# Scan inputs as two three-buffer tiles, four residual tiles and earlier loads in a four-layer transformer, LoRA, Mamba and mixture-of-experts kernel

## The chip, the cores and the metric

The kernel runs on one core of one Trainium2 chip. The metric is the device time of one execution in microseconds (us), shown as the median of several executions. A profile is one further execution, recorded by the hardware profiler. Its span reaches from the first to the last recorded instruction.

## The reference, cut to what matters

The input is 4 sequences of 1024 tokens with 256 features, all float32. Four blocks follow each other, each as `x = x + layernorm(f(layernorm(x)))`:

```
f1: x*16 + position; 4 layers of linear attention (16 heads) and a 256-1024-256 feed-forward; final layernorm
f2: x @ W.T + LoRA mixture of 8 experts of rank 16, gated by a softmax
f3: Mamba: xz = x @ W_in (256 -> 2 x 512); causal conv of 4 taps; silu;
    delta = softplus(dt @ W_dt + b);   per channel d and state s (16):
    h[t] = h[t-1] * exp(delta[t,d] * A[d,s]) + (delta*u)[t,d] * B[t,s];   y[t,d] = sum_s h[t] * C[t,s]
    y = (y + xc * D) * silu(z);  out = layernorm(x + y @ W_out)
f4: top-1 mixture of 8 experts (256-1024-256), 320 slots each
```

The recurrence over `t` is the scan that this document is about. It is done for 4 sequences x 512 channels x 16 states.

## The kernel before, in words

**Tiling.** The tokens are cut into 8 blocks of 512 (`TB`), two blocks to a sequence. A block of activations is a tile of 128 partitions x 4 x 256 (512 KB, 4 KB a partition). 32 units (block, layer) of the transformer run as a software pipeline: the loop at L1279 goes over steps `u`, and in each step it calls parts of several units: `a_norm`, `a_turn`, `a_query`, `a_keys` for unit u+3, `a_sums` for u+2, `b_heads`, `b_turn`, `b_out`, `b_turn2` for u+1, and `f_up`, `f_down` for u. Two sequences are in work at a time, so up to four blocks hold a residual tile `X[j]`. When a block has passed its last layer, `c_norm` (u-1) reads `X[j]` for the last time, and `c_add` to `c_open` do the LoRA part. `init(j)` (L281), called at the start of step u for unit u+4 when that unit is of layer 0, loads the input `xt` and the position table `pos`, normalizes `xt`, and makes `X[j]` (L288, five buffers, tag "X"). `a_norm` for that unit comes one step later.

**Between the parts** `pump` (L1268) draws pieces of a second stream, with a credit of 34 to 42 per step: for each block `front(j)` (Mamba's projections, the convolution, delta; stores to DRAM), `scan(j)`, `back(j)` (the output projection), `route(j)`, and near the end the experts. When the steps are over, what is left of the stream runs alone.

**Front.** `turn` (L698) transposes the block, then `project(0)` and `project(1)` (L710) each take a buffer of tag "t4" (three buffers), load half of `w_in` (512 KB, L712) and multiply at once (L716). L763 to L795 compute delta and delta*u and store them as `dud` in DRAM, one after the other for each channel.

**Scan.** 128 partitions are 16 channels x 8 states, so a block has 32 groups of 16 channels, each with two halves of the states (k = 0, 1). For each group one DMA (L842, issued on SP's queue) reads 16 channels of `dud` and repeats each over 8 partitions into `dd`, 128 x 2 x 512: delta in `dd[:, 0]`, delta*u in `dd[:, 1]`. Tag "dd" has two buffers; in the last two blocks every third group takes the free weight buffer "wkv" in its place. Then for each k: GpSimd (POOL) multiplies `dbu = dd[:, 1] * B` (L848, three buffers), ScalarE (ACT) does `h = exp(A * dd[:, 0])` into PSUM (L850, two buffers), VectorE (DVE) runs the scan instruction (L854), saves the last column (L858) and multiplies by C (`hc`, L860, nine buffers), and TensorE (PE) sums over the states (L818). The `dd` buffer is free when both POOL and ACT have read it for k = 1.

**Experts.** Every second expert holds its two halves of w1, and every expert its result `ye`, in buffers of tag "X".

**What sets the order.** A scheduler of the framework puts the instructions of each engine into one fixed order when the kernel is built: it takes what is ready in its own estimate, earliest in the program first, and gives out the buffers in that order. On the chip each engine works through its order strictly, and so does SP, which issues nearly all DMAs: an instruction or a DMA that waits holds up all that stand behind it in its queue.

Of the kernel before, what the change touches and what calls it, by code (L numbers as in the profile page):

```python
# [17 lines left out]
P = 128  # L18
D = 256
# [47 lines left out]
def sandwich_kernel(ctx: ExitStack, tc: tile.TileContext, io: dict):  # L67
# [145 lines left out]
    def layers(ctx: ExitStack):  # L213
# [64 lines left out]

        X = {}

        def init(j):  # L281

            xt = tok(f"xt{j}")
            nc.sync.dma_start(xt, xblock(x_in, j))
            pos = tok(f"pos{j}")
            nc.sync.dma_start(pos, xblock(io["pos"], j % NB))
            norm_on_act(xt, xt)
            X[j] = xres.tile([P, NT, D], F32, tag="X", name="X", bufs=5)  # L288
            nc.vector.scalar_tensor_tensor(X[j], xt, math.sqrt(D), pos, ALU.mult, ALU.add)

        S = [dict() for _ in units]
        KV = {}
# [402 lines left out]
        def front(j):  # L695

            mcol = m["mcol"]
            uT = turn(closed.pop(j), pool=fpool, tag="t4", bufs=3)  # L698
            yield 0
            xc = fpool.tile([P, NDB, TB], F32, tag="xc", name="xc")  # L700
            stores = []

            def store(dst, src):
                stores.append((dst, src))

            def flush():
                while stores:
                    nc.sync.dma_start(*stores.pop(0))

            def project(part):  # L710
                w = fpool.tile([P, NC_D, D_IN], F32, tag="t4", name="win", bufs=3)
                nc.sync.dma_start(w, io["w_in"][:, :, part * D_IN : (part + 1) * D_IN])  # L712
                for db in range(NDB):
                    ps = mm([P, TB], "psx")
                    for kc in range(NC_D):
                        nc.tensor.matmul(  # L716
                            ps,
                            w[:, kc, db * P : (db + 1) * P],
                            uT[:, kc, :],
                            start=kc == 0,  # L720
                            stop=kc == NC_D - 1,
                        )
                    yield db, ps

            def sigmoid(src):

                s = fpool.tile([P, TB], F32, tag="sg", name="sg", bufs=2)
                nc.scalar.activation(s, src, AF.Exp, scale=-1.0)
                nc.scalar.activation(s, s, AF.Ln, bias=1.0)
                nc.scalar.activation(s, s, AF.Exp, scale=-1.0)  # L730
                return s

            for db, ps in project(0):
                w = mcol[:, db, M_W : M_W + 4]
                xi = fpool.tile([P, TB + 3], F32, tag="xi", name="xi")
                if j % NB == 0:
                    nc.gpsimd.memset(xi[:, 0:3], 0.0)
                else:
                    nc.gpsimd.tensor_copy(xi[:, 0:3], m["hist"][:, db, :])
                nc.scalar.copy(xi[:, 3 : TB + 3], ps)  # L740
                nc.scalar.activation(
                    ps, ps, AF.Identity, bias=mcol[:, db, M_CB : M_CB + 1], scale=w[:, 3:4]
                )
                if j % NB == 0:
                    nc.gpsimd.tensor_copy(m["hist"][:, db, :], xi[:, TB : TB + 3])
                for k in range(3):
                    nc.vector.scalar_tensor_tensor(
                        ps, xi[:, k : k + TB], w[:, k : k + 1], ps, ALU.mult, ALU.add
                    )
                s = sigmoid(ps)  # L750
                nc.vector.tensor_tensor(xc[:, db, :], s, ps, ALU.mult)
                store(xcd[j][db], xc[:, db, :])
                yield 2.1
                flush()
            for db, ps in project(1):
                s = sigmoid(ps)
                nc.vector.tensor_tensor(s, s, ps, ALU.mult)
                store(zsd[j][db], s)
                yield 0.8
                flush()  # L760
            ps = mm([P, TB], "psd")
            for c in range(NDB):
                nc.tensor.matmul(  # L763
                    ps, m["w_x"][:, c, :], xc[:, c, :], start=c == 0, stop=c == NDB - 1
                )
            dbc = fpool.tile([P, TB], F32, tag="dbc", name="dbc")
            nc.scalar.copy(dbc, ps)
            for side in range(2):
                for h in range(NSH):
                    r = side * 32 + DT_RANK + h * SH  # L770
                    store(bcd[j][side, :, h, :], dbc[r : r + SH, :])
            yield 0
            flush()


            for db in range(NDB):
                ps = mm([P, TB], "psdt")
                o = db * 32
                nc.tensor.matmul(
                    ps, m["w_dt"][o : o + DT_RANK, :], dbc[o : o + DT_RANK, :], start=True, stop=True  # L780
                )
                bdt = mcol[:, db, M_BDT : M_BDT + 1]
                du = fpool.tile([P, 2, TB], F32, tag="t4", name="du", bufs=3)
                e, lv = du[:, 0, :], du[:, 1, :]
                v1 = fpool.tile([P, TB], F32, tag="sg", name="v1", bufs=2)
                nc.scalar.activation(e, ps, AF.Abs, bias=bdt)
                nc.scalar.activation(ps, ps, AF.Relu, bias=bdt)
                nc.scalar.activation(e, e, AF.Exp, scale=-1.0)
                nc.scalar.activation(lv, e, AF.Ln, bias=1.0)
                nc.vector.tensor_scalar(v1, e, 1.0, -1.0, ALU.add, ALU.add)  # L790
                nc.gpsimd.tensor_tensor(v1, e, v1, ALU.subtract)
                nc.gpsimd.tensor_tensor(v1, v1, lv, ALU.add)
                nc.vector.tensor_tensor(ps, v1, ps, ALU.add)
                nc.scalar.copy(du[:, 0, :], ps)
                nc.vector.tensor_tensor(du[:, 1, :], xc[:, db, :], ps, ALU.mult)  # L795
                store(dud[j][db], du)
                yield 2
                flush()

        def scan(j):  # L800
# [12 lines left out]
            for db in range(NDB):  # L813
# [13 lines left out]
                for r in range(GQ):  # L827
# [6 lines left out]
                    for q in range(4):  # L834
                        g = q * GQ + r
                        gg = db * (P // GC) + g
                        if j >= NBLK - 2 and g % 3 == 2:

                            dd = wpool.tile([P, 2, TB], F32, tag="wkv", name="dd")
                        else:  # L840
                            dd = spool.tile([P, 2, TB], F32, tag="dd", name="dd", bufs=2)
                        nc.sync.dma_start(  # L842
                            dd,
                            dud[j][db][g * GC : (g + 1) * GC].unsqueeze(1).to_broadcast([GC, SH, 2, TB]),
                        )
                        for k in range(NSH):
                            dbu = spool.tile([P, TB], F32, tag="dbu", name="dbu", bufs=3)
                            nc.gpsimd.tensor_tensor(dbu, dd[:, 1, :], Bt[:, k, :], ALU.mult)  # L848
                            h = ps_h.tile([P, TB], F32, tag="h", name="h")
                            nc.scalar.activation(  # L850
                                h, dd[:, 0, :], AF.Exp, scale=m["A"][:, gg, k : k + 1]
                            )
                            last = m["last_h"][:, gg, k : k + 1]
                            nc.vector.tensor_tensor_scan(  # L854
# [199 lines left out]
        def expert(k, e=None):  # L1054
# [12 lines left out]
                row = e * CAP  # L1067
                which = slice(e, e + 1)
            if k % 2:
                w1 = [xres.tile([P, NC_D, FF // 2], F32, tag="X", name="ew1", bufs=5) for _ in range(2)]  # L1070
                w2 = apool.tile([P, NFC, D], F32, tag="kv", name="ew2", bufs=1)
            else:
                w1 = [wpool.tile([P, NC_D, FF // 2], F32, tag=t, name="ew1") for t in ("w1a", "w1b")]
                w2 = wpool.tile([P, NFC, D], F32, tag="w2", name="ew2")
# [33 lines left out]
            for f in range(NFC):  # L1108
# [11 lines left out]
                nc.scalar.activation(hT[-1][:, f % 4, :], ps, AF.Relu)  # L1120
                if f % 2:
                    yield 0
            ye = xres.tile([P, NCK, D], F32, tag="X", name="ye", bufs=5)
            both = mm([P, 2, D], "pse")
            last = ps_kv.tile([P, NC_D, P + 1], F32, tag="kv", name="psk").rearrange(
                "p c m -> p (c m)"
# [150 lines left out]
        init(0)  # L1277
        load(0, "cols", "wq", "wkv", "rkv")
        for u in range(-3, len(units) + 4):  # L1279
            if at(u + 4) and u > -4 and units[u + 4][1] == 0:  # L1280
                init(units[u + 4][2])
            if u == 2:
                load_lora()
            if u == 4:
# [3 lines left out]
            def add(func, n, *args, when=at):  # L1288
                if when(n):
                    parts.append(lambda: func(n, *args))  # L1290

            add(a_norm, u + 3)
            add(a_sums, u + 2)
            add(f_up, u, 0)
            add(c_norm, u - 1, when=last_layer)
            add(c_open, u - 3, when=last_layer)
            parts.append(lambda: load(u + 1, "w1a"))
            add(b_heads, u + 1)
# [16 lines left out]
            parts.append(lambda: load(u + 4, "cols", "wq", "wkv", "rkv"))  # L1315
            add(c_gate, u - 1, when=last_layer)
            add(b_turn2, u + 1)
            for part in parts:
                part()
                pump(SSM_RATE[min(len(begun), 2)] / len(parts))  # L1320
# [110 lines left out]
```

## Time and profile before

| | |
|---|---|
| median of 3 executions | 2957.96 us (2955.56 to 2959.54) |
| the profiled execution's own time | 2954.41 us |
| its span | 2952.6 us |
| mean granted TensorE clock | 0.910 |
| PE busy | 2459.1 us (83%) |
| DVE busy | 1867.6 us (63%) |
| ACT busy | 1541.6 us (52%) |
| POOL busy | 1121.7 us (38%) |
| first and last scan instruction (DVE L854) | 801.7 and 2922.6 us |
| last matmul of the transformer (PE L494) | 2388.5 us |

How to read it: 800 us belong to the transformer alone, then the scans run beside the transformer until about 2400 us, and the rest is scans and experts. Busy time is that of an engine's own instructions; on POOL it is rough. A line of a group gives, after the count, the busy time, the mean duration in ns, and the idle time of the engine just before these instructions with what ended it. A line of waits reads "who, at which line <- what ended the wait: us in total, times, longest us". "SPq" is SP's queue of DMA issues.

### The profile page before, as it was taken

The page shows a single profiled execution, that of the slowest core. Times are in us where ns is not written, and L with a number is a line of the kernel's source. Part 1 is how long each engine was busy: PE and PEld are TensorE (multiplying, and loading weights), DVE is VectorE, ACT ScalarE, POOL GpSimd, SP SyncE. Part 2 cuts the span into 40 slices and gives each one's busy share as a digit, 9 for nine tenths or more (in the row PEclk, how much of TensorE's full clock was granted, in tenths as well). Part 3 has the DMA queues.
Part 4 walks back from the last instruction along what each step waited for, and adds up shares of the span by engine and source line. Part 5 has one row for each costly group of instructions (what it writes and reads, how often), then busy time and mean ns, then how long its engine had stood idle before and what let it go on. Part 6 is the DMA issues. An engine that isn't in the chain of part 4 may idle for free. (4 is left out here: it accounts for less than half of the span.)

```text
span 2952.6 us, 30274 instructions
## 1 busy us (share of the span) xinstructions
PE 2459.1 (83%) x9172; PEld 1467.1 (50%) x9172; DVE 1867.6 (63%) x4182; ACT 1541.6 (52%) x3213; POOL 1121.7 (38%) x878
## 2 busy tenths in 40 slices
PE   5978899988799999888889988986886874787776
PEld 3646566656455555545545545543443432344443
DVE  3122332333487577785358878787887885688787
ACT  4434544445555665454556655664564544655443
POOL 0000010112243345452135365444554563456664
PEclk9989999989999999999899999997997986899888
DMA  4011111112344254452244445555455352866663
GB/s 111 22 66 50 29 50 37 59 60 75 101 143 121 87 157 126 116 137 67 76 144 136 129 137 159 145 146 154 118 146 147 104 148 75 244 182 195 163 195 78
DMA packets 165353, 342.05 MB, mean 116 GB/s; under 512 B 28101, under 2 KB 75418, under 8 KB 162112
## 3 DMA queue, kind: packets, MB, share of 16 engines
q1 hardware_dynamic: 160896, 334.78, 39.1%
q0 software_dynamic: 4288, 5.27, 1.0%
q8 instruction: 75, 1.23, 0.2%
q14 instruction: 94, 0.77, 0.1%
HBM read 281.13 MB, written 59.92 MB: 116 GB/s over the span
## 5 line engine op out<-in xcount | busy, mean ns | idle before, releaser
L848 POOL TENSOR_TENSOR dbu<-dd,bc 128x512 f32<-128x512 f32 x512 | 656.5, 1315 | 575.4 <-DMA dd<-dud 300.0
L850 ACT ACTIVATE h<-dd,A 128x512 f32<-128x512 f32 x512 | 347.0, 689 | 406.6 <-DVE hc L860 358.5
L494 PE MATMUL ps<-w,fT 128*128 128x256 f32 x2048 | 471.2, 389 | 20.0 <-DVE du L795 7.1
L494 PEld LDWEIGHTS ps<-w,fT 128*128 128x128 f32 x2048 | 397.7, 196 | 96.6 <-DVE qT L342 11.1
L860 DVE TENSOR_TENSOR hc<-h,bc 128x512 f32<-128x512 f32 x512 | 342.5, 678 | 19.9 <-PE y L818 15.6
L854 DVE TENSOR_TENSOR_SCAN h<-h,last_h,dbu 128x512 f32<-128x512 f32 x256 | 322.3, 1277 | 44.8 <-ACT h L850 31.7
L854 DVE TENSOR_TENSOR_SCAN h<-h,dbu 128x512 f32<-128x512 f32 x256 | 308.1, 1219 | 37.9 <-POOL dbu L848 21.8
L818 PE MATMUL y<-hc,gsum 128*32 128x512 f32 x1024 | 246.9, 660 | 93.1 <-DVE hc L860 86.5
L475 PE MATMUL psf<-hT,w1b 128*128 128x512 f32 x512 | 239.1, 621 | 16.9 <-DVE att L429 8.7
L475 PE MATMUL psf<-hT,w1a 128*128 128x512 f32 x512 | 240.8, 617 | 11.4 <-ACT hT L305 11.1
L482 ACT ACTIVATE fT<-psf,cols 128x512 f32<-128x512 f32 x256 | 171.6, 679 | 117.5 <-PE psf L475 117.1
L355 PE MATMUL pskv<-wkv,hT 128*128 128x512 f32 x512 | 227.1, 594 | 6.3 <-DVE qT L342 2.4
L460 POOL TENSOR_TENSOR X<-X,ro 128x1024 f32<-128x1024 f32 x32 | 75.4, 2358 | 335.1 <-ACT nrm L151 335.0
L716 PE MATMUL psx<-t,win 128*128 128x512 f32 x256 | 139.3, 681 | 42.8 <-DMA win<-in_w_in_dram 25.2
L475 PEld LDWEIGHTS psf<-hT,w1b 128*128 128x128 f32 x512 | 99.8, 199 | 147.5 <-issue 138.5
L475 PEld LDWEIGHTS psf<-hT,w1a 128*128 128x128 f32 x512 | 96.2, 197 | 134.0 <-issue 83.7
L115 ACT ACTIVATE r<-mv,eps 128x4 f32<-128x4 f32 (+1 forms) x105 | 30.8, 294 | 246.9 <-DVE mv L131 246.0
L355 PEld LDWEIGHTS pskv<-wkv,hT 128*128 128x128 f32 x512 | 96.3, 190 | 124.5 <-issue 101.5
L818 PEld LDWEIGHTS y<-hc,gsum 128*32 128x32 f32 x1024 | 38.9, 113 | 215.6 <-DVE hc L860 137.0
L502 DVE TENSOR_TENSOR X<-X,ps 128x512 f32<-128x512 f32 x64 | 43.5, 679 | 154.9 <-PE ps L494 154.9
L300 PE MATMUL pt<-ident,nrm 128*128 128x128 f32 x512 | 83.7, 305 | 68.5 <-ACT nrm L187 27.0
L332 PE MATMUL psq<-hT,wq 128*128 128x512 f32 x256 | 123.9, 626 | 11.0 <-DVE X L456 6.4
(217 smaller groups left out, 4147.2 us busy)
## 6 DMA issues: line engine op xcount, KB each, us to landing
dd<-dud SPq DMA_DIRECT2D x256, 512.0 KB
w<-in_w_dram SPq DMA_DIRECT2D x16, 1024.0 KB
dud<-du SPq DMA_DIRECT2D x32, 512.0 KB
xt<-in_x_dram SPq DMA_DIRECT2D x16, 512.0 KB
wkv<-in_wkv_dram SPq DMA_DIRECT2D x16, 512.0 KB
w1a<-in_w_dram SPq DMA_DIRECT2D x16, 512.0 KB
w1b<-in_w_dram SPq DMA_DIRECT2D x16, 512.0 KB
win<-in_w_in_dram SPq DMA_DIRECT2D x16, 512.0 KB
```

Source lines behind the costliest of these rows:

```text
L300: nc.tensor.transpose(pt[:, i, :], src[:, i, c * P : (c + 1) * P], ident)
L332: nc.tensor.matmul(ps, w["wq"][:, kc, mc * P : (mc + 1) * P], hT[:, kc, :], start=kc == 0, stop=kc == NC_D - 1,)
L355: nc.tensor.matmul(ps, hT[:, kc, i * P : (i + 1) * P], w["wkv"][:, kc, :], start=kc == 0, stop=kc == NC_D - 1,)
L475: nc.tensor.matmul(ps, w["w1b" if part else "w1a"][:, kc, k * P : (k + 1) * P], hT[:, kc, :], start=kc == 0, stop=kc == NC_D - 1,)
L482: nc.scalar.activation(fT[:, k, :], ps, AF.Relu, bias=w["cols"][:, C_BF + f : C_BF + f + 1])
L494: nc.tensor.matmul(ps[:, k, :], S[u]["fT", f // (NFC // 2)][:, f % (NFC // 2), i * P : (i + 1) * P], w["w2"][:, f, :], start=f == 0, stop= ...
L716: nc.tensor.matmul(ps, w[:, kc, db * P : (db + 1) * P], uT[:, kc, :], start=kc == 0, stop=kc == NC_D - 1,)
L818: nc.tensor.matmul(y[q * 32 : (q + 1) * 32, :], m["gsum"][:, r, :], tiles[q, k], start=r == 0 and k == 0, stop=r == GQ - 1 and k == NSH - 1,)
L848: nc.gpsimd.tensor_tensor(dbu, dd[:, 1, :], Bt[:, k, :], ALU.mult)
L850: nc.scalar.activation(h, dd[:, 0, :], AF.Exp, scale=m["A"][:, gg, k : k + 1])
L854: nc.vector.tensor_tensor_scan(h, h, dbu, 0.0 if half == 0 else last, ALU.mult, ALU.add)
L860: nc.vector.tensor_tensor(hc, h, Ct[:, k, :], ALU.mult)
```

## The change

1. `dd` becomes two tiles, `dd0` (delta, read by ACT) and `dd1` (delta*u, read by POOL), 128 x 512 each, with three buffers each, filled by two DMAs of 256 KB. The loan of "wkv" in the last two blocks is dropped.
2. Tag "X" has four buffers in place of five. `init` loads and normalizes as before, but is called at the end of step u, and `X[j]` is made in a new part `a_begin` at the start of the next step, after `c_norm`, which is moved to the front of the parts.
3. `front` issues the load of the first half of `w_in` ahead of `turn`, and that of the second half after the second of the four pieces of `project(0)`.

```diff
-        def init(j):
+        begin = {}
+
+        def init(u):
+            if units[u][1]:
+                return
+            j = units[u][2]
...
             norm_on_act(xt, xt)
-            X[j] = xres.tile([P, NT, D], F32, tag="X", name="X", bufs=5)
-            nc.vector.scalar_tensor_tensor(X[j], xt, math.sqrt(D), pos, ALU.mult, ALU.add)
+            begin[j] = xt, pos
+
+        def a_begin(u):
+            j = units[u][2]
+            if units[u][1] == 0:
+                xt, pos = begin.pop(j)
+                X[j] = xres.tile([P, NT, D], F32, tag="X", name="X", bufs=4)
+                nc.vector.scalar_tensor_tensor(X[j], xt, math.sqrt(D), pos, ALU.mult, ALU.add)
...
+            w_in = [load_in(0)]
+            yield 0
             uT = turn(closed.pop(j), pool=fpool, tag="t4", bufs=3)
...
-            for db, ps in project(0):
+            for db, ps in project(w_in[0]):
...
                 flush()
-            for db, ps in project(1):
+                if db == 1:
+                    w_in.append(load_in(1))
+            for db, ps in project(w_in[1]):
...
-                        if j >= NBLK - 2 and g % 3 == 2:
-
-                            dd = wpool.tile([P, 2, TB], F32, tag="wkv", name="dd")
-                        else:
-                            dd = spool.tile([P, 2, TB], F32, tag="dd", name="dd", bufs=2)
-                        nc.sync.dma_start(
-                            dd,
-                            dud[j][db][g * GC : (g + 1) * GC].unsqueeze(1).to_broadcast([GC, SH, 2, TB]),
-                        )
+                        dd = []
+                        for k in range(2):
+                            t = spool.tile([P, TB], F32, tag=f"dd{k}", name=f"dd{k}", bufs=3)
+                            nc.sync.dma_start(
+                                t,
+                                dud[j][db][g * GC : (g + 1) * GC, k, :].unsqueeze(1).to_broadcast([GC, SH, TB]),
+                            )
+                            dd.append(t)
                         for k in range(NSH):
...
-                            nc.gpsimd.tensor_tensor(dbu, dd[:, 1, :], Bt[:, k, :], ALU.mult)
+                            nc.gpsimd.tensor_tensor(dbu, dd[1], Bt[:, k, :], ALU.mult)
...
-                                h, dd[:, 0, :], AF.Exp, scale=m["A"][:, gg, k : k + 1]
+                                h, dd[0], AF.Exp, scale=m["A"][:, gg, k : k + 1]
...
-            if at(u + 4) and u > -4 and units[u + 4][1] == 0:
-                init(units[u + 4][2])
...
+            add(c_norm, u - 1, when=last_layer)
+            add(a_begin, u + 3)
             add(a_norm, u + 3)
             add(a_sums, u + 2)
             add(f_up, u, 0)
-            add(c_norm, u - 1, when=last_layer)
...
             add(b_turn2, u + 1)
+            if u > -4:
+                add(init, u + 4)
```

More of the change, by code (lines that the diff above doesn't have):

```diff
@@ L697, in front, with load_in @@
             mcol = m["mcol"]
+            def load_in(part):
+                w = fpool.tile([P, NC_D, D_IN], F32, tag="t4", name="win", bufs=3)
+                nc.sync.dma_start(w, io["w_in"][:, :, part * D_IN : (part + 1) * D_IN])
+                return w
+            w_in = [load_in(0)]
+            yield 0
             uT = turn(closed.pop(j), pool=fpool, tag="t4", bufs=3)
@@ L708, in flush, with project @@
                     nc.sync.dma_start(*stores.pop(0))
-            def project(part):
-                w = fpool.tile([P, NC_D, D_IN], F32, tag="t4", name="win", bufs=3)
-                nc.sync.dma_start(w, io["w_in"][:, :, part * D_IN : (part + 1) * D_IN])
+            def project(w):
                 for db in range(NDB):
@@ L1069, in expert @@
             if k % 2:
-                w1 = [xres.tile([P, NC_D, FF // 2], F32, tag="X", name="ew1", bufs=5) for _ in range(2)]
+                w1 = [xres.tile([P, NC_D, FF // 2], F32, tag="X", name="ew1", bufs=4) for _ in range(2)]
                 w2 = apool.tile([P, NFC, D], F32, tag="kv", name="ew2", bufs=1)
@@ L1122, in expert @@
                     yield 0
-            ye = xres.tile([P, NCK, D], F32, tag="X", name="ye", bufs=5)
+            ye = xres.tile([P, NCK, D], F32, tag="X", name="ye", bufs=4)
             both = mm([P, 2, D], "pse")
```

## The prediction

> **What bounds the kernel now.** I read the page first, then the busy time by stage, the waits of the engines, those of SP's queue, and the trace around three places. By stage (start:end in us, then PE, PEld, DVE, ACT and POOL busy):
>
> ```profile
> 800.00:1340.00 540.00, 486.97 (x1917) 288.31 (x1917) 412.52 (x838) 311.88 (x638) 246.66 (x188) 0.96 0.44 125
> 1520.00:2030.00 510.00, 442.96 (x1704) 255.28 (x1700) 412.80 (x865) 309.58 (x611) 258.68 (x204) 0.95 0.50 145
> 2030.00:2450.00 420.00, 320.33 (x1160) 175.51 (x1160) 345.94 (x710) 213.70 (x404) 231.19 (x179) 0.85 0.48 132
> 2450.00:2953.00 503.00, 360.97 (x1243) 196.62 (x1241) 368.43 (x706) 246.78 (x540) 258.05 (x208) 0.83 0.59 163
> ```
>
> No engine is full. Up to 1340 PE leads (90%, DVE 76%), to 2030 it is PE 87% and DVE 81%, then DVE 82% and PE 76%. Both work through fixed orders, so what is lost is lost in waits of one for the other. The page's groups for the scan show where its input is late:
>
> ```profile
> L848 POOL TENSOR_TENSOR dbu<-dd,bc 128x512 f32<-128x512 f32 x512 | 656.5, 1315 | 575.4 <-DMA dd<-dud 300.0
> L850 ACT ACTIVATE h<-dd,A 128x512 f32<-128x512 f32 x512 | 347.0, 689 | 406.6 <-DVE hc L860 358.5
> L854 DVE TENSOR_TENSOR_SCAN h<-h,last_h,dbu 128x512 f32<-128x512 f32 x256 | 322.3, 1277 | 44.8 <-ACT h L850 31.7
> L854 DVE TENSOR_TENSOR_SCAN h<-h,dbu 128x512 f32<-128x512 f32 x256 | 308.1, 1219 | 37.9 <-POOL dbu L848 21.8
> ```
>
> POOL waits 300.0 us for `dd`, but the scans, which follow, find DVE idle for 44.8 + 37.9 us only. Most of POOL's wait is slack. The waits of all engines and of SP's queue:
>
> ```profile
> POOL dbu L848 <- DMA dd<-dud: 300.0, 113, 9.5
> DVE psdt L793 <- POOL v L792: 58.9, 26, 6.7
> ACT h L850 <- DMA dd<-dud: 41.8, 18, 6.5
> PE psx L716 <- DMA win<-in_w_in_dram: 25.2, 6, 6.1
> ```
>
> ```profile
> SPq L842 <- ACT h L850: 713.2, 199, 10.9
> SPq L842 <- POOL dbu L848: 34.1, 42, 2.6
> ```
>
> SP stands 713 us at the issue of a `dd` until ACT has read the buffer. Laying the trace's releases beside the issues, 215 of 256 `dd` DMAs start within 1 us of the release of their buffer; they hold 248 of POOL's 300 us. From issue to the last packet a `dd` takes 3.87 us (median), and POOL starts 0.95 us later. So two buffers are the cause, not bandwidth.
>
> **What the Trainium skill says.** "DMA: Bandwidth & Descriptors", Anatomy of one DMA: DMA engines do not wait on semaphores; the issuing sequencer does, before dispatch. The 713 us agree. Its fit, given there for DMAs from GpSimd, is about 2.0 us + bytes / 436 GB/s: an estimate of 3.2 us for 512 KB and 2.6 us for 256 KB. From SP this trace has 3.87 us for `dd` and 2.37 us for `xl` (256 KB, same row length as a new half); I use the trace. Same page, Rules for kernel authors: few large transfers are better than many small ones, with 64 KB as the size below which overhead rules. The halves stay above. "Perfetto Trace Analysis", GPSIMD Engine Instruction: POOL's spans are unreliable, start-to-start is better. It agrees: two `dbu` in a row fill 2.50 us, 1.25 each, where the group's mean is 1.315.
>
> **Part 1: the start.** In the order of the changed kernel the load of block 1 stands in SP's queue behind 8 of the 32 small loads of A, and its statistics on DVE stand behind `kva` (L372 of before) of block 0. The trace of before here:
>
> ```profile
> 27.73 13.92 SPq L662 DMA_DIRECT2D A<-alog  x32
> 40.09 1.23 DVE L372 SCALAR_TENSOR_TENSOR kva<-kva,ke 128x1024 f32<-128x1024 f32 x1 [2.47 <-ACT ke L371]
> 45.27 1.92 PE L300 MATMUL pt<-ident,nrm 128*128 128x128 f32 x8
> ```
>
> Gain: block 0's `a_norm` no longer shares ACT with block 1. From X at 11.57: four L171 at 0.40, four L176 at 0.49, 0.5 for L115 and L116, 0.75 on DVE, 0.74 until PE starts: 17.3 in place of 20.66, 3.3 us earlier. So `kva` ends at 41.3 - 3.3 = 38.0. Loss: block 1's chain then starts. In the trace block 0 takes 6.46 us from first statistics (5.11) to X (11.57) and, as just counted, 5.7 us to PE: 38.0 + 6.5 + 5.7 = 50.2 in place of 45.27. **+5 us**, and PE has nothing else in its order there. The load is not what is late: the 8 loads take 8 x 0.435 = 3.5 us, so it is issued near 30 and needs 3.9 us as before, 4 us ahead of 38. If that cover is gone, each us is one us.
>
> For block 2 (its X at 292 before) the order puts `X` between the sums of attention and their scaling, and `a_turn` of block 2 ahead of `b_out`. PE gains 2.1 us (its wait for `nrm` at 292.5) and 2.0 us (`kvm` was behind statistics that waited for `xt`), so psa ends at 317.6 in place of 321.7; then 0.4 for the last sums, 1.2 for X, 5.7 for `a_norm`, 1.1 for two copies on ACT between, 1.2 for the transposes: `b_out` at 327.2, before 325.3. **+2 us.** For blocks 3 to 7 the chain from the block's last addition through `c_norm` (6.4 us), X (1.2) and `a_norm` (5.7), 13 us, or 19 with eight activations of `f_up` (0.68 each) in between, runs beside `f_up` twice (7 us each), `b_heads` (2 to 4) and `b_turn` (1), 17 to 19 us of PE, and later scan work. I put 0; uncovered it is up to 10 us a block. Experts with four X buffers: their loads stand at the same places between the experts and wait for PE as before: 0.
>
> **Part 2: w_in.** The trace of SP's queue and PE:
>
> ```profile
> 728.88 0.55 SPq L273 DMA_DIRECT2D w1a<-in_w_dram  x1
> 729.48 0.60 SPq L712 DMA_DIRECT2D win<-in_w_in_dram  x1
> 735.50 5.56 PE L716 MATMUL psx<-t,win 128*128 128x512 f32 x8 [5.78 <-DMA win<-in_w_in_dram]
> 762.53 3.95 PE L716 MATMUL psx<-t,win 128*128 128x512 f32 x5 [4.69 <-DMA win<-in_w_in_dram]
> ```
>
> `win` waited behind `w1a`, which waited for PE. In the new order it stands ahead of `w1a` for blocks 0 and 2, right after a load issued 12 us earlier: 5.8 + 6.1 us of PE's wait go. The second half still stands behind `w1b` and `cols`, and moves past one store only: from 757.66 to some 756.5, 1.2 us, twice. `w1a` is later by the 0.6 us of one issue; its user comes a step later. Together **-14 us**. At 735 and 1460 PE has no more work in its order, and no scan runs, so I count it whole; bounds 9 and 18.
>
> **Part 3: dd.** Removed: 256 DMAs of 512 KB. Added: 512 of 256 KB. SP pays 256 x 0.52 us = 133 us more, out of time it stood waiting (713). Packets: 128 x 4 KB took 1.99 us of sixteen engines; the broadcast loads with 2 KB rows (`rkv`, `ro`, `gb`) took 0.92 to 0.98 for 256 KB: the same, 1.9 us. The second half is issued 0.5 us later. Behind a waiting `dd` stand stores and weights; with a buffer more it waits less. With three buffers a load starts one group (6 to 8.6 us) earlier, more than the 3.87 + 0.95 us it takes, so the 248 us should go and the other 52 stay. Where does it come out? While `dd` was waited for, DVE was idle 39 us by the trace (idle stretches laid over one another). So 83% of 39 = 32 us at DVE, of which some 15 of the 39 lie before 1340, where PE leads: I count 24 x 0.83 = **-20 us**. Upper bound: add the 29 us of DVE idle in which POOL was computing a late `dbu`, 68 us. Lower bound: below zero, +8: if all 113 waits instead grow by 0.6 us, 68 us of POOL, of which DVE sees 39 of 312. In the last 500 us DVE lost under 2 us to `dd`, so the tail stays.
>
> **Sum.** Profiled execution, span 2952.6 and 1.8 around it: 2954.4 + 5 + 2 - 14 - 20 = 2927. The median shown lies 3.5 above it: 2957.96 - 27 = 2931 us.
>
> **Rivals.** (A) `dd` is hidden anyway: POOL's wait vanishes, DVE and PE then wait for each other. For it: only 83 us of idle before 512 scans. Part 3 gives 5: 2946. (B) The wait comes out in full: late `v` behind `dbu` in POOL's queue costs DVE 58.9 us (line above), and PE waits 86.5 us for `hc`. Part 3 gives 55: 2896. (C) Slower: the begin of blocks 4 to 7, now tied to `c_norm` of the unit four before it, is not covered, and PE waits at `pt<-nrm` for ACT, 10 us or more a block, with blocks' tiles (`xt`, `pos`) held longer in a pool of four: 2958 + 7 - 14 - 5 + 40 = 2986. Against it: the 17 us of PE work in between. It decides from 7 us a block, when 4 x 7 has eaten the 27. (D) That a third buffer isn't used, because SP stands behind other waits, is A's number.
>
> **How the numbers follow.** Forecast 0.42, A 0.25, B 0.13, C 0.20. Where the scheduler's new order adds or takes single waits (one of 24.8 us stands in the tail now), each case spreads by some 12 us. A measurement can tell about 0.2%, 6 us. Faster (below 2952): 0.38 + 0.16 + 0.13 = 0.67; within: 0.03 + 0.06 + 0.02 = 0.11; slower: 0.01 + 0.03 + 0.18 = 0.22. Range 2890 to 2980: from B's near end to part of C. The forecast's own range is 2915 to 2948.
>
> **What would show it.** POOL's wait for `dd` near 50 us and SP's wait for ACT at `dd` well below 713; PE's wait for `win` near 10; second `pt<-nrm` on PE near 50 us; idle of DVE before L854 below 60. I am wrong if the scans per group are no shorter (8.6, 8.0, 7.1, 7.8, 6.0, 6.0 us in the first six blocks), or if PE waits at `pt<-nrm` for the begun blocks.

## The result and the profile after

The changed kernel takes 2907.39 us (median of 4, 2901.54 to 2909.93). The kernel before, run beside it, takes 2956.76 us (median of 4). The ratio is 0.9832, 95% interval 0.9812 to 0.9851: 49 us faster (44 to 56). The profiled execution took 2901.54 us, its span is 2899.8 us and the mean granted TensorE clock 0.916.

The scan's groups on the page of the changed kernel, to be laid beside L848, L850 and L854 of before:

```profile
L866 POOL TENSOR_TENSOR dbu<-dd,bc 128x512 f32<-128x512 f32 x512 | 657.0, 1314 | 525.3 <-DVE h L872 306.3
L868 ACT ACTIVATE h<-dd,A 128x512 f32<-128x512 f32 x512 | 346.8, 688 | 372.5 <-DVE hc L878 351.4
L872 DVE TENSOR_TENSOR_SCAN h<-h,last_h,dbu 128x512 f32<-128x512 f32 x256 | 321.9, 1277 | 33.3 <-ACT h L868 19.1
L872 DVE TENSOR_TENSOR_SCAN h<-h,dbu 128x512 f32<-128x512 f32 x256 | 307.7, 1219 | 26.4 <-ACT h L868 16.7
```

POOL is idle for nearly as long as before (525.3 us, before 575.4). Only what ends its idle time has changed: it now waits for a free `dbu` buffer, which the scan gives back, and no longer for `dd`. That is slack. DVE's idle time ahead of the scans fell from 82.7 to 59.7 us.

The waits of the engines, and those of SP's queue:

```profile
POOL dbu L866 <- DMA dd<-dud: 27.9, 12, 4.9
...
PE psx L733 <- DMA win<-in_w_in_dram: 10.9, 2, 5.9
```

```profile
SPq L859 <- POOL dbu L866: 479.6, 200, 10.5
SPq L859 <- ACT h L868: 214.9, 115, 6.8
```

The `dd` wait is gone (300.0 to 27.9), and so is most of that for `win` (25.2 to 10.9). SP stands as long at the `dd` issue as before (694.5 us, before 747.3), but one group further ahead, so nobody sees it. The size of that wait never was a measure of its cost.

The start and the first `w_in`, from the trace of the changed kernel:

```profile
49.41 2.17 PE L311 MATMUL pt<-ident,nrm 128*128 128x128 f32 x8 [8.20 <-ACT nrm L187]
...
721.06 0.56 SPq L712 DMA_DIRECT2D win<-in_w_in_dram  x1
732.67 0.54 SPq L273 DMA_DIRECT2D w1a<-in_w_dram  x1
733.89 3.70 PE L733 MATMUL psx<-t,win 128*128 128x512 f32 x8 [0.38 <-ACT t L314]
```

PE comes to the second `pt<-nrm` at 49.41 us (before 45.27): the start is later, as forecast. `win` is issued 11.6 us ahead of `w1a`, and PE's wait of 5.78 us at `psx` is 0.38 us.

To see where the 49 us come from I cut both traces at the same pieces of work, the last feed-forward addition (`X<-X,ps`) of five units. Columns: start:end and length in us, then PE, PEld, DVE, ACT and POOL busy, PE's clock, DMA share, GB/s. Before:

```profile
824.00:1357.00 533.00, 488.87 (x1944) 291.69 (x1943) 399.77 (x817) 302.35 (x618) 237.94 (x179) 0.97 0.42 121
...
1546.00:1951.00 405.00, 363.46 (x1449) 217.75 (x1448) 332.52 (x726) 242.62 (x484) 209.75 (x159) 0.96 0.49 141
1951.00:2399.00 448.00, 345.20 (x1236) 185.58 (x1235) 361.76 (x708) 243.14 (x457) 234.08 (x192) 0.88 0.49 136
2399.00:2953.00 554.00, 394.10 (x1353) 210.93 (x1351) 412.12 (x801) 269.19 (x585) 286.15 (x228) 0.81 0.58 161
```

After:

```profile
818.00:1313.00 495.00, 474.00 (x1905) 284.33 (x1904) 392.06 (x799) 299.65 (x613) 237.42 (x180) 0.99 0.41 128
...
1505.00:1907.00 402.00, 361.72 (x1447) 217.79 (x1446) 334.60 (x727) 242.62 (x483) 208.48 (x158) 0.96 0.45 139
1907.00:2354.00 447.00, 347.71 (x1239) 188.48 (x1239) 366.87 (x705) 243.84 (x459) 234.65 (x191) 0.87 0.44 136
2354.00:2900.00 546.00, 387.59 (x1350) 208.02 (x1349) 415.44 (x803) 267.77 (x584) 287.94 (x229) 0.83 0.55 163
```

38 of the 52.8 us of span are won in the first stage, where PE leads, and 8 in the tail. The stages from 1546 to 2399, from which I had expected 20, give 4. (A small part of the first stage's gain is moved work: the begin of the last two blocks, `X` at 1230.7 and 1307.5 before, stands at 1271.2 and 1355.8 after, partly in the next stage, not shown, which takes 192 us in place of 189 with 36 more matmuls and 5.7 us more of PE busy time.)

### The profile page after: what moved, and what is told of

Its sections match the earlier page's. It is cut to its first block, busy times and chain, and to the rows that moved or that the text cites. A ratio compares the mean times of both kernels' runs of the same rounds, so it can differ in the third digit from the quotient of the medians.

```text
span 2899.8 us, 30694 instructions
## 1 busy us (share of the span) xinstructions
PE 2441.7 (84%) x9172; PEld 1460.7 (50%) x9172; DVE 1871.0 (65%) x4182; ACT 1541.2 (53%) x3213; POOL 1125.8 (39%) x878
## 5 line engine op out<-in xcount | busy, mean ns | idle before, releaser
L866 POOL TENSOR_TENSOR dbu<-dd,bc 128x512 f32<-128x512 f32 x512 | 657.0, 1314 | 525.3 <-DVE h L872 306.3
L505 PE MATMUL ps<-w,fT 128*128 128x256 f32 x2048 | 464.0, 385 | 3.0 <-ACT fT L493 2.1
L837 PE MATMUL y<-hc,gsum 128*32 128x512 f32 x1024 | 241.0, 650 | 73.5 <-DVE hc L878 67.5
L486 PE MATMUL psf<-hT,w1a 128*128 128x512 f32 x512 | 241.1, 618 | 10.9 <-ACT hT L316 7.1
L115 ACT ACTIVATE r<-mv,eps 128x4 f32<-128x4 f32 (+1 forms) x105 | 30.7, 293 | 264.2 <-DVE mv L131 263.3
L733 PE MATMUL psx<-t,win 128*128 128x512 f32 x256 | 133.5, 651 | 24.8 <-DMA win<-in_w_in_dram 10.9
```

Source lines behind the costliest of these rows:

```text
L486: nc.tensor.matmul(ps, w["w1b" if part else "w1a"][:, kc, k * P : (k + 1) * P], hT[:, kc, :], start=kc == 0, stop=kc == NC_D - 1,)
L505: nc.tensor.matmul(ps[:, k, :], S[u]["fT", f // (NFC // 2)][:, f % (NFC // 2), i * P : (i + 1) * P], w["w2"][:, f, :], start=f == 0, stop= ...
L733: nc.tensor.matmul(ps, w[:, kc, db * P : (db + 1) * P], uT[:, kc, :], start=kc == 0, stop=kc == NC_D - 1,)
L837: nc.tensor.matmul(y[q * 32 : (q + 1) * 32, :], m["gsum"][:, r, :], tiles[q, k], start=r == 0 and k == 0, stop=r == GQ - 1 and k == NSH - 1,)
L866: nc.gpsimd.tensor_tensor(dbu, dd[1], Bt[:, k, :], ALU.mult)
```

## The experiments

One word first, since several runs turn on it: the scheduler of the framework makes a new order for each kernel. With `dd` as before in the changed kernel (x_win), the traces show at 300 of the 9172 places of PE's matmuls and at 517 of the 4182 places in DVE's order an instruction on other tiles than in the changed kernel, though both kernels do the same work. A run that takes a part away changes both the part and the order.

Ratios are to the kernel before, run beside it. The us are the ratio's distance from 1, times 2955 us.

| run | median, us | ratio (95%) | us against before |
|---|---|---|---|
| win_only | 2948.84 | 0.9993 (0.9978 to 1.0007) | -2 |
| x_only | 2940.18 | 0.9968 (0.9956 to 0.9980) | -9 |
| split2 | 2955.48 | 1.0015 (1.0001 to 1.0030) | +4 |
| before_noload | 2965.54 | 1.0049 (1.0034 to 1.0063) | +14 |
| x_win | 2945.85 | 0.9971 (0.9960 to 0.9981) | -9 |
| x_dd | 2926.09 | 0.9886 (0.9869 to 0.9903) | -34 |
| one3 | 2927.72 | 0.9900 (0.9883 to 0.9917) | -30 |
| split_win | 2946.82 | 0.9959 (0.9943 to 0.9974) | -12 |
| late_same_order | 2946.25 | 0.9975 (0.9962 to 0.9988) | -7 |
| dd_other_order | 2937.18 | 0.9930 (0.9905 to 0.9954) | -21 |
| one3_same_order | 2906.54 | 0.9827 (0.9802 to 0.9853) | -51 |
| early1 | 2893.73 | 0.9789 (0.9764 to 0.9814) | -62 |
| the changed kernel | 2907.39 | 0.9832 (0.9812 to 0.9851) | -50 |

### First: each part alone

My theory from the two profiles was that `dd`'s third buffer gives its gain before 1357 us. The rivals were the other parts, the split without a third buffer, and the order.

**win_only**

```diff
+            w_in = [load_in(0)]
+            yield 0
...
+                if db == 1:
+                    w_in.append(load_in(1))
```

> The kernel before with nothing changed but the loads of the two w_in tiles, issued early as in the changed kernel. My theory (the prediction's part 2): PE's wait for win goes from 25.2 us to near 10, -14 us (9 to 18) against before, and the scans stay as long as before. Rival (the gain of the whole change sits here, because a freer SP queue brings the rest with it): -30 us or more, and POOL's wait for dd falls from 300 us too. Rival (the wait is only moved to the next late thing): within 5 us of before.

PE's wait for `win` fell to 14.4 us, much as expected, and the time did not follow: -2 us (-7 to +2). The profiled execution is 6 us ahead of before at 824 us and 28 at 1747, and only 7 at 2123. The gain stands where the prediction put it: from the end of unit 10 to that of unit 11 the run is 7 us shorter than before, and from unit 19 to unit 21 8 us. In another order something later took it back; this run alone does not tell what.

**x_only**

```diff
+        begin = {}
+        def init(u):
...
+            begin[j] = xt, pos
+        def a_begin(u):
...
+                X[j] = xres.tile([P, NT, D], F32, tag="X", name="X", bufs=4)
...
+            add(c_norm, u - 1, when=last_layer)
+            add(a_begin, u + 3)
```

> The kernel before with the four X buffers, the begin of a block split into its load and its X, and the moved c_norm; dd and w_in as before. The prediction's part 1 says +7 us (start +5, block 2 +2, blocks 3 to 7 nil). From the comparison of the two traces I now expect +3: start +5, block 2 +4, blocks 4 and 5 -6. Rival (the new order itself gives the gain between 800 and 1357 us, where part 3 counted nothing): -20 us or less, with shorter scans of blocks 0 and 1. Rival C of the prediction: +20 us or more, with PE waiting at pt<-nrm in the begins of blocks 4 to 7.

-9 us (-13 to -6). In its trace the start costs 5.2 us and block 2 another 6.2. Then it wins: 5 us to the unit that ended at 646 before, 5 to that of 824, and 14 to that of 1433, where it is 12 ahead; it ends 12 ahead. The stage from 824 to 1433 is 595 us long, with 551.2 of PE busy, in place of 609 and 553.8. Rival C did not come; the rival of the new order has the right place and less than the size.

**split2**

```diff
+                        dd = []
+                        for k in range(2):
+                            t = spool.tile([P, TB], F32, tag=f"dd{k}", name=f"dd{k}", bufs=2)
...
```

> The kernel before with dd as two tiles of two buffers each (no third buffer, and without the borrowed wkv buffer of the last two blocks). If the separate release by POOL and by ACT is what helps: most of the gain, -25 us or more, POOL's wait for dd below 100 us. My theory (the third buffer is what helps): within 10 us of before, POOL's wait for dd above 200 us, since each half still starts only when its own buffer, two groups old, is read; ACT waits for the first half as late as before. If the doubled number of DMAs costs something by itself, it shows here as slower: 0 to +8 us.

A surprise. The waits for `dd` in it:

```profile
POOL dbu L847 <- DMA dd<-dud: 46.1, 26, 5.5
ACT h L849 <- DMA dd<-dud: 44.4, 19, 5.1
```

The split alone takes POOL's wait from 300.0 to 46.1 us, which I had given to the third buffer: the half for POOL comes free when POOL has read it, and no longer when ACT has. ACT's wait for its half stays, 44.4 us where it was 41.8, as I had expected of ACT; with three buffers it is 17.8 us (changed kernel), 15.5 (x_dd) and 17.0 (one3). A scan needs what POOL makes and what ACT makes, and DVE is idle before the scans for as long as before (84.6 us, before 82.7). And the time does not fall: +4 us (0 to 9). This looks like rival A of the prediction, POOL's wait goes and what it hid stays; but with two buffers `dd` is still late for ACT. Whether that or the order of this kernel keeps the time up, no run tells.

**before_noload**

```diff
+                        if (j, db) not in kept:
+                            kept[j, db] = fpool.tile([P, 2, TB], F32, tag="ddk", name="ddk")
...
+                        dd = kept[j, db]
```

> The kernel before with dd loaded once for each 16 groups (one channel block of a block) and kept, in place of once a group: it leaves out 15 of 16 loads, so all groups use the same channels' delta, and the values of the scan are others. It bounds what the lateness of dd costs in the kernel before, with the traffic of the loads and their place in SP's queue. My theory (dd costs some 40 us before 1357 us and hardly anything after): -35 to -50 us, scans of blocks 0 and 1 near 7.5 us a group as in the changed kernel, those of blocks 4 to 7 within 0.3 us of before. The prediction's part 3 (20 us, all of it after 1340): -20 to -30, the scans of blocks 2 to 5 shorter. Rival A (dd is hidden anyway): within 10 us of before.

This was to bound the cost of `dd`, and it does not. The edit makes one load for each 8 groups, 32 in all, and not one for each 16, as I had written. The pool has one buffer for a tag, so that each of the 32 loads left could start only when the last group of the load before it had been read. POOL still waits for them 20 times, 113.8 us in all and up to 10.4 us, each time at the first group of a channel block, and SP stands up to 37.4 us at one load with all else behind it. It is no bound of anything.

### Second: pairs

**x_win**

```diff
-                            t = spool.tile([P, TB], F32, tag=f"dd{k}", name=f"dd{k}", bufs=3)
+                            dd = spool.tile([P, 2, TB], F32, tag="dd", name="dd", bufs=2)
...
```

> The changed kernel with dd as before: one tile of two buffers, loaded by one DMA, with the loan of wkv in the last two blocks. The X part alone gave -11 us against before, the w_in part alone -2, two buffers each for two tiles +4. If parts add: -13 us against before here, and the third buffer of dd carries the other 36 us (the last part of my theory). If the parts do not add (rival: the framework's scheduler builds another order for each kernel, and the changed kernel's order of PE's instructions is a lucky one, dd or not): -30 us or more here.

-9 us. The parts add here as far as I can tell, and the `dd` part of the changed kernel, in whatever order comes with it, is worth 0.9971 - 0.9832 = 1.4%, 41 us.

**x_dd**

```diff
-            w_in = [load_in(0)]
-            yield 0
...
-            for db, ps in project(w_in[0]):
+            for db, ps in project(0):
```

> The changed kernel with the two w_in loads where they were before. If parts add: the changed kernel's -49 us less what w_in alone gave (-2), so -47 us against before. The prediction's part 2: -35. If the gain is an effect of the parts together: -25 us or less.

-34 us, as by the prediction's part 2. The early `w_in` is worth 16 us in the changed kernel (0.9886 to 0.9832, +-8), 17 with two split tiles (split2 to split_win), and nothing where POOL waits for `dd` (-2 on before, +1 on x_only), each with an order of its own. Yet in all four pairs the traces have its gain at the two places that the prediction named: 5 to 7 us between the ends of units 10 and 11, and 5 to 8 between those of units 19 and 21. On before and on x_only the later stages lose it again; on x_only the tail alone loses 16 us (550 to 566).

**one3**

```diff
-                        for k in range(2):
-                            t = spool.tile([P, TB], F32, tag=f"dd{k}", name=f"dd{k}", bufs=3)
+                        dd = spool.tile([P, 2, TB], F32, tag="dd", name="dd", bufs=3)
...
```

> The changed kernel with dd as one tile with three buffers, loaded by one DMA of 512 KB. If the third buffer is what helps: as the changed kernel, -45 to -50 us against before, POOL's wait for dd below 60 us. If the split is what helps (each half is released by its own reader): -13 us, as without the dd part.

-30 us, between the two. POOL's wait is 57.9 us and ACT's 17.0, so the third buffer without the split takes both away, and still 20 us are missing.

**split_win**

```diff
+            w_in = [load_in(0)]
...
+                            t = spool.tile([P, TB], F32, tag=f"dd{k}", name=f"dd{k}", bufs=2)
```

> The kernel before with the early w_in loads and dd as two tiles of two buffers each; X as before. The split alone took POOL's wait for dd from 300 to 46 us and gave nothing (+4 us). If parts add: +2 us against before. If what dd's wait holds back shows only when w_in is no longer late as well (PE's next limit): -15 us or more.

-12 us (-17 to -8): the two parts do not add (+2). ACT's wait for `dd` is 54.5 us in it. Of the four kernels in which POOL hardly waits for `dd`, the two with two buffers lay at +4 and -12 us, and the two with three (one3, x_dd) at -30 and -34. x_dd lacks the early `w_in`, but one3 lacks only the split, POOL and ACT hardly wait for `dd` in it, and still it lay 20 us above the changed kernel. The waits could not be all of it.

### Third: waits and order apart

A kernel can be held to an order: an edge is added from each instruction of PE, DVE, ACT and POOL to the one that shall follow it, with no semaphore behind it. The order is read from another built kernel. The traces show it kept: late_same_order and one3_same_order have the changed kernel's instructions at all places of these four engines, and dd_other_order those of x_win. SP's order of DMA issues was left free; in dd_other_order it differs from the changed kernel's at 92 of 1088 places, so that what is called order below includes a share of SP's. (Line numbers of these kernels are some 80 higher.)

```diff
+        for eng, steps in order_of.items():
...
+                    tc.add_manual_dep(
+                        mine[at_], last_.name,
+                        mybir.DependencyInfo(mybir.DependencyClass.NoSync, mybir.DependencyReason.DATA),
+                        reason="order",
+                    )
```

**late_same_order** is x_win held in the order of the changed kernel. Order as after, loads as before.

> dd as before (one tile, two buffers, with the loan) in the changed kernel, and the instructions of PE, DVE, ACT and POOL held by added edges in exactly the order that they have in the changed kernel; only SP's order is free. It has the late dd and not the other order. If the waits for dd are what the third buffer takes away: -9 us against before, as the same kernel with the scheduler's own order. If the gain of the dd part is the order that the scheduler makes when it reckons with three buffers: -50 us, as the changed kernel. My theory after eight runs: mostly waits up to 2400 us (some 20 us) and mostly order in the tail (another 20): -28 us.

**dd_other_order** is the changed kernel held in the order of x_win. Loads as after, order as for two buffers.

> The changed kernel, dd with its two tiles of three buffers, with the instructions of PE, DVE, ACT and POOL held in the order that they have in the kernel with dd as before. It has the early dd and not the changed kernel's own order. If waits for dd are all: -50 us against before. If order is all: -9 us. My theory: -30 us, with the scan of the last block as long as with dd as before (6.1 us a group) and the units up to 2400 us as early as in the changed kernel.

**one3_same_order** is one3 held in the order of the changed kernel.

> dd as one tile with three buffers, with the instructions of the four engines held in the changed kernel's order. With its own order it gave -29 us against before. If the split itself is of use on the chip (two halves, each free when its own reader is done, and 1.5 us sooner there): -29 us here too. If the split only led the scheduler to a better order: -50 us. My theory: the latter, -45 us or more.

Together they make a square (us against before):

| | order made for a late `dd` (x_win) | order of the changed kernel |
|---|---|---|
| `dd` late, two buffers | -9 | -7 |
| `dd` early, three buffers | -21 | -50, one tile -51 |

Neither is the cause alone. In the order made for two buffers the early loads are worth 12 us (0.9971 to 0.9930, some +-8). In the order of the changed kernel they are worth 42 (0.9975 to 0.9832, +-7; to one3_same_order 44). That order without the early loads is worth nothing (+1, +-5), with them 29 (+-9). Two of my three expectations, those between the extremes, missed: late_same_order (-28 expected, -7 measured) came out at the end, and dd_other_order (-30, -21) nearer to it than I thought. one3_same_order came as expected. One3's missing 20 us were order: in the changed kernel's order one tile is as good as two, so the split does nothing on the chip that the third buffer does not do.

The lengths of the same stages show where (start, then the five of above, last line: span; us, from the windows of each trace). Each column is one execution, and executions of one kernel lie 8 to 23 us apart, so that a difference of a few us in one stage tells nothing by itself:

| | before | x_win | dd_other_order | late_same_order | one3_same_order | after |
|---|---|---|---|---|---|---|
| to unit 11 | 824 | 817 | 821 | 822 | 820 | 818 |
| PE leads, blocks 0 and 1 | 533 | 505 | 501 | 511 | 494 | 495 |
| no scan | 189 | 192 | 193 | 193 | 192 | 192 |
| blocks 2 and 3 | 405 | 412 | 410 | 417 | 407 | 402 |
| blocks 4 and 5 | 448 | 447 | 448 | 449 | 443 | 447 |
| tail | 554 | 566 | 564 | 555 | 548 | 546 |
| span | 2953 | 2939 | 2937 | 2947 | 2904 | 2900 |

Of the 38 us that the change wins in the first stage, 22 are there with a late `dd` too (533 to 511 in late_same_order, 505 in x_win): they come with the other parts and their order.

In the changed kernel's order a late `dd` costs 16 us in the first scan stage, 10 to 15 with blocks 2 and 3, and 7 to 9 in the tail; in the order for two buffers 4, 2 and 2. The tail has a share of order besides: 566 to 555 with a late `dd`, 564 to 546 with an early one. (From the first scan of the last block to the end of its 16th are 64.7 and 65.1 us in x_win and dd_other_order, and 52.0, 48.4 and 48.9 in the three others.) That share does not go with the number of buffers: in the last block a group takes 6.1 us in x_win, in dd_other_order and in one3, which has three buffers, but 5.6 and 5.8 in before and split2, which have two. What the square calls an order is one order that the scheduler happened to make, not what two or three buffers must give.

How the wait reaches PE can be read because both kernels have the same order. Windows of the first scan stage, late_same_order:

```profile
822.00:1333.00 511.00, 477.44 (x1900) 283.90 (x1900) 396.14 (x798) 299.97 (x613) 236.55 (x180) 0.98 0.43 123
```

and one3_same_order:

```profile
820.00:1314.00 494.00, 473.34 (x1901) 283.34 (x1901) 393.90 (x798) 299.73 (x613) 237.72 (x180) 0.98 0.45 127
```

Of 17 us, 13 are PE's idle time (511 - 477.4 = 33.6, 494 - 473.3 = 20.7) and 4 its busy time. PE's waits in these windows, late_same_order:

```profile
PE pt L391 <- DVE kva L453: 4.9, 3, 3.8
PE psf L566 <- DVE att L520: 4.6, 2, 2.4
PE pskv L446 <- DVE X L593: 4.3, 2, 2.1
PE y L917 <- DVE hc L959: 3.9, 2, 2.8
```

and one3_same_order:

```profile
PE y L917 <- DVE hc L955: 3.1, 2, 2.2
PE psf L566 <- DVE att L520: 2.3, 1, 2.3
PE pt L391 <- DVE kva L453: 2.1, 2, 1.5
PE pskv L446 <- DVE X L593: 1.2, 1, 1.2
```

PE does not wait longer for the scan's own `hc` (3.9, 3.1). It waits for `kva`, `att` and `X`, the transformer's pieces on DVE: 13.8 us in place of 5.6, which is 8 of the 13 us. They stand behind scans in DVE's fixed order, and a scan that waits for a late `dbu` holds them. The longest of these waits, in the trace of late_same_order:

```profile
879.15 2.49 POOL L947 TENSOR_TENSOR dbu<-dd,bc 128x512 f32<-128x512 f32 x2 [4.93 <-DMA dd<-dud]
887.50 1.23 DVE L953 TENSOR_TENSOR_SCAN h<-h,dbu 128x512 f32<-128x512 f32 x1 [2.79 <-POOL dbu L947]
888.64 0.68 DVE L453 TENSOR_TENSOR kva<-pskv,rkv 128x512 f32<-128x512 f32 x1
889.38 0.91 PE L391 MATMUL pt<-ident,nrm 128*128 128x128 f32 x4 [3.76 <-DVE kva L453]
```

POOL waits 4.93 us for `dd`, which delays its next `dbu`, behind two of its transformer pieces, to 886.22; the scan waits for that, `kva` stands behind the scan, and PE waits 3.76 us. At the same place one3_same_order has PE waiting 1.49 us. (In the two windows DVE's idle time at the scans is 20.3 and 14.7 us; at `psdt<-v`, whose `v` stands behind `dbu` on POOL, 15.1 and 10.6).

### Fourth: a better version

**early1**

```diff
         init(0)
+        init(1)
...
-            if u > -4:
+            if u > -3:
```

> The changed kernel with the load and the statistics of block 1 ahead of the loop, right after block 0's, as in the kernel before; its X is still made where the change put it. Prediction's part 1: the 5 us of the start are the late load of block 1, so the first unit ends at 120 in place of 125 us and the time falls by 4 to 5 us against the changed kernel, -54 us against before. Rival: block 1's statistics then delay block 0's own on ACT as they did before (3.3 us), and 1 or 2 us are gained. Rival: the new order of the scheduler costs or gives up to 12 us elsewhere, with the start gained all the same.

PE at the second `pt<-nrm`, trace of early1:

```profile
43.55 1.91 PE L311 MATMUL pt<-ident,nrm 128*128 128x128 f32 x8
```

It is there at 43.55 in place of 49.41 us, and the first unit ends at 117.6 in place of 125.3. The time is 2893.73 us: -62 us against before, and some 12 us below the changed kernel (0.9789 beside 0.9832, and beside 0.9827 for one3_same_order). The intervals overlap a little, and the profiled execution of early1, the second slowest of its six, has a span only 2.1 us below that of the changed kernel's profiled execution, the fastest of its four. That it is faster is likely by the medians; by how much is not settled. It has the lowest median of the study, with the start gained as the prediction's part 1 reads it.

## Why the prediction was right and wrong

The sum, -27 us, had the right sign and about half the size. By its own steps:

- **Part 1, the start, +5**: +5.3 at the first unit's end, and early1 shows the cause as told, block 1's statistics behind `kva`: with them ahead, 7.7 us come back. The trace of the change has the steps too: PE's first `pt` at 17.38 us (17.3 forecast), `kva` done at 37.3 (38.0), the second `pt` at 49.41 (50.2). (The items given for 17.3 add up to 17.1.) **Block 2, +2**: +3.7 (6.0 to 9.7), mis-sized, and 6.2 in x_only.
- **Part 1, blocks 3 to 7, counted at 0**: wrong. x_only gives -9 us in all where I summed +7, so at least 16 us are won after block 2. Its trace has them between 578 and 1433 us; from 824 on, PE's idle time is 43.8 us in place of 55.2. Which edit of the part does it (four buffers, the later `X`, `c_norm` first, or only another share of `pump` between more parts) was not taken apart.
- **Part 2, w_in, -14**: right in the changed kernel (-16, +-8), and the two stretches where it was to come are 12 to 15 us shorter in all four pairs of runs. That it stays to the end was luck in part: on before and on x_only the later stages took it back, and no run held the order for this part.
- **Part 3, dd, -20**: 41 to 44 measured. The step that failed is "some 15 of the 39 lie before 1340, where PE leads: I count 24 x 0.83". I took a leading PE to mean that DVE's idle time costs nothing. But PE leads with waits of its own for DVE's pieces of the transformer, which stand behind the scans. In the same order the stage that I counted at nil gave 16 us. "The tail stays" failed too: 7 to 9 us. The stages that I did count, blocks 2 to 5, gave 16 to 17 in the same order, which looks like my 20; but that order with a late `dd` takes 417 us for blocks 2 and 3 where the kernel before takes 405, so that against before only 4 are left.
- **The figure of 39 us**, DVE's idle time while POOL or ACT waits for `dd`, was better than what I made of it. In the changed kernel's order it is 52 us with a late `dd` and 7 with an early one (late_same_order and one3_same_order), 45 less, and the time falls by 44. 18 of the 52 lie in the first stage, where PE leads; they go to nil, and the stage is 17 us shorter. So taking 15 of the 39 off was the error. But it is not a measure for every order: from x_win to dd_other_order it falls from 47 to 15 us and the time by 12 only.
- **Two buffers are the cause**: it stands, with a piece that I had not thought of. The split with two buffers takes POOL's wait away, but not ACT's (44.4 us), and gives no time.
- **What I had not reckoned with at all**: that the number of buffers goes into the order. I gave the order a spread of 12 us, as chance. It is worth 29 us here, and only with the early loads. About half of that is the tail, whose slow order one3 has with three buffers and before has not with two, so that chance is not ruled out. That the scheduler, reckoning with three buffers, puts the scan's pieces where early loads can feed them is a guess that no run shows. Why its order for one3 is worse than that for two tiles of three, the runs do not say either.
- **Rivals.** A looks right for split2, where ACT's wait stays, and is wrong for the change. B had part 3's size nearly right (55), with a part of its mechanism: `v` behind `dbu` (15.1 to 10.6 us in the first scan stage), though over the whole kernel DVE's wait for `v` did not fall (58.9 to 63.0). The other part, PE's wait for `hc`, fell from 86.5 to 67.5 us, at the same order from 86.4 to 71.9 (one3_same_order), outside the first stage. C, slower by uncovered begins, did not occur.

The signs that I named came as named: `dd` wait 27.9 (near 50), SP's wait for ACT 214.9 (well below 713), `win` 10.9 (near 10), `pt<-nrm` 49.4 (near 50), idle time of DVE before the scans 59.7 (below 60). They were right while much of the gain was elsewhere. Only the scans per group told it: 8.6, 8.0, 7.1, 7.8, 6.0, 6.0 us in the first six blocks became 7.5, 7.7, 6.9, 7.8, 5.9, 6.0: shorter in the first two, hardly in those I had counted.

## What to carry to other kernels

Where a framework orders the instructions, a buffer more changes the order as well as the waits, and what one is worth depends on the other (12 or 42 us for the early loads here): hold the order fixed when you ask what a wait costs. An engine that leads is not for that reason deaf to another's waits; look at what stands behind the waiting instruction in the other engine's queue. And a wait that vanishes on one engine (300 us on POOL with the split alone) shows that an edit took hold, not that it pays: look whether the consumer behind it waits less.

## What the hardware showed besides

A PE wait can cost more than its length. In the kernel before, the recorded clock falls to half for 10.2, 6.8 and 13.7 us within 824 to 1357 us, each time from within a stretch in which PE is idle, for 6.3, 4.6 and 3.9 us. Windows in and after the first of them (the clock is the number after POOL's count):

```profile
894.00:902.00 8.00, 4.80 (x6) 2.19 (x7) 3.70 (x5) 3.65 (x5) 4.98 (x5) 0.50 0.17 41
904.00:912.00 8.00, 8.00 (x37) 3.98 (x36) 3.68 (x11) 6.67 (x18) 0.27 (x2) 1.00 0.09 33
```

In it four `psx` matmuls take 3.78 us, at full clock 1.88. The Trainium skill, "TensorE: Matmul & The Clock Gate", Part 1, tells of the halved clock after an idle window of some 3.4 us. These three pieces agree, and last two to four such windows; but the changed kernel has three pieces of 3.4 us at half clock in its first stage, from 885, 1107 and 1274 us, where the longest idle stretch of PE in the whole stage is 2.3 us. Ahead of them stand waits of up to 1.7, 1.9 and 2.3 us. At half speed are 30.7 us of that stage before and 12.6 after, 23.3 in late_same_order and 16.2 in one3_same_order. Of the last two the difference, 7.0 us at half speed, makes an estimate of 3.5 us, near the 4 us of PE busy time found above.
